# The opening of a gated, quantised feed-forward block: order of its loads, of one scale's range and of one weight tile's turns

## The chip, the cores and the metric

The kernel runs on one core of one Trainium2 chip. A core has a matrix engine (TensorE, PE in the profile), a vector engine (VectorE, DVE), a scalar engine for activation functions (ScalarE, ACT), a general engine (GpSimd, POOL) and SyncE (SP), which here only issues transfers. The engines run their own instruction streams in order and wait for each other through semaphores; transfers (DMA) run on 16 DMA engines of the core and are issued from the queue of SP or ACT. The metric is the time of one execution in microseconds (us) on the device, lower is better.

## The reference

x is (4, 1024, 512), cond is (4, 128); the weights are norm_w (512, 128), up_w (4096, 512) and down_w (512, 2048). All is float32.

```python
scale = cond @ norm_w.T + 1.0
ms = jnp.mean(x * x, axis=-1, keepdims=True)
h = x * (scale[:, None, :] * jax.lax.rsqrt(ms + EPS))
u = h @ up_w.T
val, gate = jnp.split(u, 2, axis=-1)
h = val * jax.nn.gelu(gate, approximate=False)
hq = act_quant(h)        # per token: round(h * 127 / max|h|), scaled back
wq = weight_quant(down_w) # round(w / mean|w|) in {-1, 0, 1}, scaled back
y = hq @ wq.T
return y + x
```

(`act_quant` and `weight_quant` stand in the reference inside a stop_gradient form, which leaves these values.) So each of the four batches has a scale per feature from its own row of cond; each token has a root of its mean square; the product with up_w is in full float32 precision, the product with down_w is of small whole numbers.

## The kernel before

**Products.** The up product is made of float16 parts: every float32 operand is brought into range by a power of two and split into a high and a low float16, and three of the four cross products are added in PSUM. Batches 1 to 3 use a seven-product scheme on 2 x 2 blocks (L474); batch 0, with which the kernel starts, uses the plain product (`plain`, L489, and for its very first block `plain_first`, L531), since the sums of weights that the scheme needs are made on the way. up_w is handled in 16 tiles W0 to W15 of 128 gate rows and 128 value rows. A tile is loaded (`w_load`, L248), its rows' largest values are brought to a power of two (`w_range`, L253 to L258), the rows are scaled (`w_scale`, L267 or L269), turned by TensorE against the identity (`w_turn`, L277, four 128 x 128 blocks per half) and split into high (`w_high`, ScalarE, L290 to L293) and low (`w_low`, VectorE, L299 to L302). `w_evac` (L306) keeps a float32 copy for the sums. The gate half of a tile goes ahead of its value half.

**The start.** The first half of batch 0 is four tiles of 128 tokens, `X0`. SP issues, in this order, two loads of two x tiles each (L705), W0 and W1 as four loads, two more pairs of x tiles, W2. ScalarE's queue issues cond, as one row of 4 x 128 numbers (L697), and norm_w (L698). Then:

- TensorE spreads cond's row over 128 partitions by a product with ones (`cond_spread_rows`, L159), into two PSUM tiles: the first batch's 128 numbers, and the other 384, which ScalarE copies to `cb` (L774) for a later use (`cond_scale_rest`, L175).
- VectorE multiplies norm_w by the first batch's row and adds along it, feature block by feature block (`cond_scale`, L164), adds 1 (L180) and takes the largest magnitude per partition (`cond_largest`, L182). `cond_over` turns this column into a row on TensorE (pm, L189), `cond_range` makes a power of two of its maximum on VectorE (L195 to L199), `cond_spread` brings that back to all partitions on TensorE (pd, L205). `cond_undo` (L209, L210) keeps it as `dx` and its reciprocal as `ux`, and `cond_bring_first` (L213) applies `ux` to the scale.
- ScalarE makes the sums of squares of the four x tiles (`first_sum`, L716) and the square root (L723); VectorE makes the reciprocal and one Newton step (`rsqrt_start`, L724 to L728). ScalarE scales tiles 0, 1 and 2 by it (`first_scale`, L733), VectorE tile 3 (L735). TensorE turns them, four blocks per tile, into four PSUM banks ptx (`first_turn`, L740). ScalarE writes the high half of each bank times the scale (`first_high`, L744), VectorE the low half (`first_low`, L748).
- Between these, TensorE runs products of zeros (`keep_warm`, pz, L756): six ahead of the spread, five behind it, five behind pm.
- Then `plain_first` runs 24 products of 512 columns for W0, in an order written out by hand, and calls `second_part` ahead of the seventh (W0's value rows turned and split, W1 scaled, the low halves of x, the load of the GELU table) and `second_slot` ahead of the seventeenth (W1 turned, W2 ranged and scaled).

Behind it come the other W tiles against both halves of batch 0, and then batches 1 to 3, whose vector and scalar work is placed by a small planner with costs (`Filler`, `SLOT_US`); the down products of a batch run among the up products of the next.

**What sets the order.** The program is recorded under a manual schedule: each engine runs its instructions in the order in which the lines above call them, so an instruction that waits holds up all that its engine has behind it. SP's loads are issued in order as well. PSUM has eight banks; pz, pm, pd and one ptx bank share the two banks of the tag "A".

Of the kernel before, what the change touches and what calls it, by code (L numbers as in the profile page):

```python
# [13 lines left out]
ALU = mybir.AluOpType  # L14
# [3 lines left out]
P = 128  # L18
# [23 lines left out]
def glu_quant_kernel(  # L42
# [10 lines left out]
    PE, ACT, DVE, POOL, SP = nc.tensor, nc.scalar, nc.vector, nc.gpsimd, nc.sync  # L53
    B, S, D = x.shape
    C = cond.shape[1]
# [3 lines left out]
    NA = TOK // P  # L59
    NK = D // P  # L60
    NJ = FF // P
    xf = x.flatten_outer_dims()
# [13 lines left out]
    ones = one.to_broadcast([P, P])  # L76
# [8 lines left out]
    H = cpool.tile([P, NSLOT, 2, TOK], F32, name="H")  # L85
# [10 lines left out]
    for n in range(0, P, 32):  # L96
        c = slice(n, n + 32)
# [35 lines left out]
    def pow2_floor(t):  # L133

        ti = t.bitcast(I32)
        DVE.tensor_scalar(ti, ti, EXPONENT, None, ALU.bitwise_and)

    def bank(tag, bufs, shape=None, name=None):
        return psum.tile(shape or [P, TOK], F32, name=name or tag, tag=tag, bufs=bufs)

    def po_bank(name, shape=None):
        return bank("po", 3, shape, name)


    scT = cpool.tile([P, NK, B], F32, name="scT")
    dx = cpool.tile([P, B], F32, name="dx")
    ux = cpool.tile([P, B], F32, name="ux")
    nw = R[:, 1, 0:512].rearrange("p (k c) -> p k c", k=NK)
    cb = R[:, 1, 512:1024].rearrange("p (b c) -> p b c", b=B)
    dots = R[:, 1, 1024 : 1024 + C]  # L150
    junk = R[:, 1, 2048:4096].rearrange("p (n d) -> p n d", d=D)

    cn = H[0:1, 3, 0, : B * C]

    def cond_spread_rows():

        pc = [bank("B", 1, name="pc_0"), bank("E", 2, name="pc_1")]
        for n, c in enumerate((slice(0, C), slice(C, B * C))):
            PE.matmul(pc[n][:, : c.stop - c.start], ones[:1, :], cn[:, c], start=True, stop=True)  # L159
        return pc  # L160

    def cond_scale(b, rows):
        for k in range(NK):
            DVE.scalar_tensor_tensor(  # L164
                dots, nw[:, k], 1.0, rows[:, :C], ALU.mult, ALU.mult, accum_out=scT[:, k, b : b + 1]
            )
# [11 lines left out]
    def cond_largest(b0, b1):  # L178
        v = scT[:, :, b0:b1]
        DVE.tensor_scalar(v, v, 1.0, None, ALU.add)  # L180
        mx = sm.tile([P, B], F32, name=f"mx_{b0}", tag="mx")[:, : b1 - b0]
        DVE.tensor_reduce(  # L182
            mx, v.rearrange("p k b -> p b k"), AX.X, ALU.max, apply_absolute_value=True
        )
        return mx

    def cond_over(mx, b0, b1, tag):
        pm = bank(tag, {"po": 3}.get(tag, 2), [B, P], f"pm_{b0}")[: b1 - b0]
        PE.transpose(pm, mx, ident)  # L189
        return pm  # L190

    def cond_range(pm, b0, b1):
        n = b1 - b0
        d4 = sm.tile([B, 1], F32, name=f"d4_{b0}", tag="d4")[:n]
        DVE.tensor_reduce(d4, pm, AX.X, ALU.max)  # L195
        DVE.tensor_scalar(d4, d4, 1e-30, None, ALU.max)
        pow2_floor(d4)
        dg = sm.tile([B, B], F32, name=f"dg_{b0}", tag="dg")[:n, :n]
        DVE.tensor_scalar(dg, ident[:n, :n], d4, 1.0 / X_UP, ALU.mult, ALU.mult)  # L199
        return dg  # L200

    def cond_spread(dg, b0, b1, tag):
        n = b1 - b0
        pd = bank(tag, {"po": 3}.get(tag, 2), [P, B], f"pd_{b0}")[:, :n]
        PE.matmul(pd, ones[:n, :], dg, start=True, stop=True)  # L205
        return pd

    def cond_undo(pd, b0, b1):
        DVE.tensor_copy(dx[:, b0:b1], pd)  # L209
        DVE.reciprocal(ux[:, b0:b1], dx[:, b0:b1])  # L210

    def cond_bring_first():
        DVE.tensor_scalar(scT[:, :, 0], scT[:, :, 0], ux[:, 0:1], None, ALU.mult)  # L213

    def cond_rows():

# [20 lines left out]
    def wn(j):  # L237
        return H[:, W_SLOT[j % 3]]
# [7 lines left out]
    def w_load(j, ts=(1, 0)):  # L246
        for t in ts:
            SP.dma_start(out=wn(j)[:, t], in_=up_v[j][:, t])  # L248

    def w_range(j, t0=0, t1=2):  # L250
        t = slice(t0, t1)
        am = sm.tile([P, 2], F32, name=f"wam_{j}_{t0}", tag="wam")[:, t]
        DVE.tensor_reduce(am, wn(j)[:, t], AX.X, ALU.max, apply_absolute_value=True)  # L253
        pow2_floor(am)
        DVE.tensor_scalar(sw[:, j, t], am, 2.0**-100, 1.0 / W_UP, ALU.max, ALU.mult)
        if j not in iv:
            iv[j] = sm.tile([P, 2], F32, name=f"iv_{j}", tag="iv", bufs=3)
        DVE.reciprocal(iv[j][:, t], sw[:, j, t])  # L258

    def w_gain(j):  # L260
        DVE.tensor_scalar(sg0[:, j, :], sw[:, j, :], dx[:, 0:1], None, ALU.mult)

    def w_scale(j, ts=(1, 0), eng=POOL):
        for t in ts:
            w, r = wn(j)[:, t], iv[j][:, t : t + 1]
            if eng is ACT:
                ACT.activation(w, w, AF.Copy, scale=r)  # L267
            else:
                eng.tensor_scalar(w, w, r, 1.0, ALU.mult, ALU.mult)  # L269

    def w_turn(j, banks=None, ts=(1, 0)):
        if j not in pw:
            pw[j] = banks or [po_bank(f"pw_{j}_{t}") for t in (1, 0)]
        for t in ts:
            n = 1 - t
            for k in range(NK):
                PE.transpose(  # L277
                    pw[j][n][:, k * P : (k + 1) * P], wn(j)[:, t, k * P : (k + 1) * P], ident
                )
# [414 lines left out]
    start_t = sm.tile([P, 1], F32, name="start_t", bufs=1)  # L694
    eps = sm.tile([P, 1], F32, name="eps", bufs=1)
    DVE.memset(eps, EPS)
    ACT.dma_start(out=cn, in_=cond.rearrange("(o b) c -> o (b c)", o=1))  # L697
    ACT.dma_start(out=nw, in_=norm_w.rearrange("(k p) c -> p k c", p=P))  # L698
    ACT.activation(start_t, one, AF.Sqrt)


    X0 = H[:, 4:8].rearrange("p s h d -> p (s h) d")

    def first_load(n):
        SP.dma_start(  # L705
            out=X0[:, n : n + 2],
            in_=xf[n * P : (n + 2) * P, :].rearrange("(s p) d -> p s d", p=P),
        )

    ssq0 = sm.tile([P, 8], F32, name="ssq0", bufs=1)  # L710
# [2 lines left out]
    def first_sum(n, eng=ACT):  # L713
        v, j, a = X0[:, n], junk[:, n % 4], ssq0[:, n : n + 1]
        if eng is ACT:
            ACT.activation(j, v, AF.Square, accum_out=a)  # L716
        else:
            eng.scalar_tensor_tensor(j, v, 1.0, v, ALU.mult, ALU.mult, accum_out=a)

    def rsqrt_start(t, y):  # L720

        z = sm.tile([P, NA], F32, name="newton", bufs=1)
        ACT.activation(z, t, AF.Sqrt, scale=1.0 / D, bias=eps)  # L723
        DVE.tensor_scalar(t, t, 1.0 / D, EPS, ALU.mult, ALU.add)  # L724
        DVE.reciprocal(y, z)
        DVE.tensor_tensor(z, y, y, ALU.mult)
        DVE.scalar_tensor_tensor(z, z, -0.5, t, ALU.mult, ALU.mult)
        DVE.scalar_tensor_tensor(y, z, 1.5, y, ALU.add, ALU.mult)  # L728
# [8 lines left out]
    def first_turn(n, pts):  # L737
        for k in range(NK):
            c = (n % NA) * P
            PE.transpose(pts[k][:, c : c + P], X0[:, n, k * P : (k + 1) * P], ident)  # L740

    def first_high(h, k, pt):
        c = slice(h * TOK, (h + 1) * TOK)
        ACT.activation(XP[:, 0, k, c], pt, AF.Copy, scale=scT[:, k, 0:1])  # L744
# [7 lines left out]
    def keep_warm(n):  # L752

        pz = bank("A", 2, name="pz")
        for i in range(n):
            PE.matmul(pz, warm[:, :P], warm, start=True, stop=True)  # L756

    first_load(0)
    first_load(2)
    w_load(0)  # L760
    w_load(1)
    first_load(4)
    first_load(6)
    w_load(2)
    keep_warm(6)
    pc = cond_spread_rows()
    keep_warm(5)
    for n in range(NA):
        first_sum(n)
    cond_scale(0, pc[0])  # L770
    mx = cond_largest(0, 1)
    pm = cond_over(mx, 0, 1, "A")
    rsqrt_start(ssq0[:, 0:NA], rs0[:, 0:NA])
    ACT.copy(cb[:, 1:].rearrange("p b c -> p (b c)"), pc[1][:, : (B - 1) * C])  # L774
    keep_warm(5)
    for n in (0, 1, 2):
        first_scale(n, ACT)
    first_scale(3, DVE)
    dg = cond_range(pm, 0, 1)
    w_range(0, 1, 2)  # L780
    w_scale(0, (1,), DVE)
    ptx = [po_bank(f"ptx_0_{k}") for k in range(3)] + [bank("A", 2, name="ptx_0_3")]
    first_turn(0, ptx)
    first_turn(3, ptx)
    pd = cond_spread(dg, 0, 1, "A")
    first_turn(1, ptx)
    first_turn(2, ptx)
    cond_undo(pd, 0, 1)
    cond_bring_first()
    w_turn(0, [bank("E", 2, name=f"pw_0_{t}") for t in (1, 0)], (1,))  # L790
    w_high(0, (1,))
    first_high(0, 0, ptx[0])
    w_range(0, 0, 1)
    w_low(0, (1,))
    w_scale(0, (0,), DVE)
    w_gain(0)
    first_high(0, 1, ptx[1])
    first_high(0, 2, ptx[2])
    first_high(0, 3, ptx[3])
    w_range(1)  # L800
    w_gain(1)
    w_scale(1, (0,))
# [142 lines left out]
    mx = cond_largest(1, B)  # L945
# [26 lines left out]
    pm = cond_over(mx, 1, B, "po")  # L972
    dg = cond_range(pm, 1, B)
# [178 lines left out]
    b = B - 1  # L1152
# [125 lines left out]
```

## Time and profile before

| | us |
|---|---|
| three runs, median | 752.07 |
| lowest, highest | 751.36, 752.24 |
| the profiled execution | 752.28 |
| its span, first to last instruction | 750.5 |
| TensorE busy | 741.7 |
| VectorE, ScalarE, GpSimd busy | 549.4, 377.5, 199.4 |
| norm_w's issue on ScalarE's queue, start | 1.29 |
| first instruction that uses norm_w (L164), start | 7.68 |
| square root of the sums (L723), start | 7.41 |
| x's turns (L740), first start | 11.81 |
| W0's gate rows' turns (L277), start | 15.10 |
| first product (L531), start | 16.97 |
| first GELU (L536), start | 23.82 |

The times of this table below the line of busy times are counted from the span's start. Each line of the profile names an engine, a line of the kernel, an operation and the tiles that it writes and reads; "idle before" is the time that the engine stood still ahead of an instruction and what ended it. An "x8" behind an instruction merges eight of them. "issue" is time in which nothing that the profile shows was waited for. The time of an execution is its span and about 1.8 us around it.

### The profile page before, as it was taken

The numbers are of one execution on the slowest core, as the hardware profiler recorded it, in microseconds if no ns is written. First come the engines' busy times: TensorE is split into PE (matmuls) and PEld (weight loads), VectorE is DVE, ScalarE is ACT, GpSimd is POOL, SyncE is SP. The second block draws the span as 40 slices with busy tenths as digits, with TensorE's granted clock in tenths as the row PEclk, the third lists the DMA queues.
The fourth block names the chain that finished last, engine by engine and source line by source line (L and its number), as shares of the span: only waits on it lengthen the run. The fifth ranks groups of instructions, "written<-read, shape, count | busy, mean of one in ns | idle before, by whom it ended". The sixth has DMA issues, their size and how long they took to land.

```text
span 750.5 us, 9573 instructions
## 1 busy us (share of the span) xinstructions
PE 741.7 (99%) x3484; PEld 344.9 (46%) x3484; DVE 549.4 (73%) x795; ACT 377.5 (50%) x618; POOL 199.4 (27%) x218
## 2 busy tenths in 40 slices
PE   7999999999999999999999999999999999999997
PEld 3554455454444444444444444444444444444443
DVE  5868688897989885545679886444778887445896
ACT  5758455656235655543434656443433666332274
POOL 0389577899010030332010030333020000000200
PEclk9999999999999999999999999999999999999999
DMA  6279649777622433666832415466823333333243
GB/s 224 71 260 233 195 156 226 202 195 172 202 84 99 130 124 119 183 204 146 228 103 98 127 64 182 137 190 179 197 99 102 109 114 109 107 99 112 88 152 112
DMA packets 94074, 111.28 MB, mean 148 GB/s; under 512 B 61382, under 2 KB 61894, under 8 KB 94028
## 3 DMA queue, kind: packets, MB, share of 16 engines
q1 hardware_dynamic: 93498, 110.42, 49.9%
q8 instruction: 27, 0.44, 0.3%
q10 hardware_dynamic: 530, 0.26, 0.1%
q14 instruction: 19, 0.16, 0.1%
HBM read 74.47 MB, written 23.09 MB: 130 GB/s over the span
## 4 chain that ended last, share of the span: by engine, by line
PE 93%; DVE 2%; ACT 2%; DMA 1%; POOL 1%; issue 1%; ACTq 0%; SPq 0%; DVEq 0%; POOLq 0%
PE A L474 32%; PE E L474 16%; PE po L682 11%; PE pg L489 9%; PE pv L489 9%; PE B L474 8%; PE po_end L682 4%; PE pw L277 2%; DMA R<-in_L_cond_norm_w_dram 1%; DMA SXY<-s_dram 1%; PE ptx L740 1%; DVE R L748 0%; DVE H L175 0%; ACT djk L356 0%; POOL SXY L325 0%
## 5 line engine op out<-in xcount | busy, mean ns | idle before, releaser
L474 PEld LDWEIGHTS <-SXY 128*128 128x128 f16 x2016 | 197.0, 98 | 238.5 <-DMA SXY<-s_dram 1.3
L474 PE MATMUL A<-R,SXY 128*128 128x512 f16 x1152 | 264.9, 379 | 0.1
L474 PE MATMUL E<-R,SXY 128*128 128x512 f16 x576 | 140.0, 379 | 0.0
L568 DVE SCALAR_TENSOR_TENSOR H<-A,sg,t 128x512 f32<-128x512 f32 x48 | 36.0, 750 | 81.1 <-PE A L474 81.1
L579 ACT ACTIVATE t<-t,sg 128x512 f32<-128x512 f32 x48 | 34.5, 720 | 106.5 <-DVE t L578 106.5
L682 PE MATMUL po<-wd,R 128*128 128x512 bf16 x384 | 85.3, 379 | 0.0
L682 PEld LDWEIGHTS <-R 128*128 128x128 bf16 x512 | 50.1, 98 | 60.4
L656 DVE TENSOR_TENSOR H<-H,am 128x1024 f32<-128x1024 f32 x64 | 76.2, 1216 | 0.0
L617 POOL PARTITION_ALL_REDUCE am<-R x8 | 14.6, 1821 | 221.1 <-DVE R L603 221.1
L601 DVE TENSOR_REDUCE gm<-H 128x512 f32<-128x1024 f32 x56 | 69.0, 1233 | 2.5 <-DMA wd<-tn 1.5
L474 PE MATMUL B<-R,SXY 128*128 128x512 f16 x288 | 70.0, 379 | 0.0
L578 DVE TENSOR_TENSOR t<-E,t 128x512 f32<-128x512 f32 x48 | 32.6, 679 | 49.3 <-PE E L474 49.3
L383 POOL TENSOR_TENSOR rs<-ssq,neghalf 128x2 f32<-128x2 f32 (+1 forms) x13 | 9.6, 739 | 205.2 <-DVE ssq L382 205.0
L489 PE MATMUL pv<-R 128*128 128x512 f16 x246 | 61.6, 379 | 0.0
L489 PE MATMUL pg<-R,SXY 128*128 128x512 f16 x252 | 57.8, 379 | 0.5 <-ACT g L536 0.5
L489 PEld LDWEIGHTS <-SXY 128*128 128x128 f16 x378 | 37.0, 98 | 42.9 <-issue 0.8
L489 PEld LDWEIGHTS <-R 128*128 128x128 f16 x366 | 35.8, 98 | 41.9 <-DVE R L299 0.2
L565 ACT ACTIVATE t<-B,sg 128x512 f32<-128x512 f32 x48 | 33.0, 687 | 37.2 <-PE B L474 37.2
L664 ACT ACTIVATE H<-H 128x1024 f32<-128x1024 f32 x39 | 40.9, 1049 | 20.8 <-DVE H L656 20.8
L549 ACT COPY t<-A 128x512 f32<-128x512 f32 x48 | 28.0, 584 | 45.0 <-PE A L474 44.7
L560 ACT COPY v<-E 128x512 f32<-128x512 f32 x48 | 28.1, 586 | 32.1 <-PE E L474 29.3
L556 ACT COPY B<-A 128x512 f32<-128x512 f32 x48 | 27.4, 571 | 31.2 <-PE A L474 30.2
(155 smaller groups left out, 911.7 us busy)
## 6 DMA issues: line engine op xcount, KB each, us to landing
SXY<-s_dram SPq DMA_DIRECT2D x48, 640.0 KB, 3.9
SXY<-s_dram SPq DMA_DIRECT2D x48, 256.0 KB, 4.6
s_dram<-SXY SPq DMA_DIRECT2D x11, 896.0 KB, 5.4
H<-in_L_cond_up_w_dram SPq DMA_DIRECT2D x32, 256.0 KB, 4.3
xr<-in_x_dram SPq DMA_DIRECT2D x19, 256.0 KB, 4.5
out_dram<-xr SPq DMA_DIRECT2D x19, 256.0 KB, 2.2
s_dram<-R SPq DMA_DIRECT2D x5, 896.0 KB
H<-in_x_dram SPq DMA_DIRECT2D x8, 512.0 KB, 5.7
```

The costliest lines, as they stand in the source:

```text
L474: PE.matmul(o, s[:, w, k, :], tv[:, :, c, l, k, :], start=start and n == 0, stop=stop and n == len(TERMS) - 1, skip_group_check=True,)
L489: PE.matmul(ps, a[k // 2][:, w, k % 2, :], XP[:, l, k, h * TOK : (h + 1) * TOK], start=n == 0, stop=n == len(terms) - 1,)
L549: ACT.copy(cur["t2"], cur["A"])
L560: ACT.copy(cur["v"], cur["E"])
L565: ACT.activation(cur["t1"], pb, AF.Gelu, scale=gain(g, 1))
L568: DVE.scalar_tensor_tensor(h_half(g - 1, 0), prev["A"], gain(g - 1, 0), prev["t1"], ALU.mult, ALU.mult)
L578: DVE.tensor_tensor(prev["t2"], prev["E"], prev["t2"], ALU.add)
L579: ACT.activation(prev["t2"], prev["t2"], AF.Gelu, scale=gain(g - 1, 1))
L601: DVE.tensor_reduce(gm[0], v, AX.X, ALU.max, apply_absolute_value=True)
L656: DVE.tensor_tensor(v, v, r.to_broadcast([P, 2, TOK]), ALU.mult)
L664: ACT.activation(v, v, AF.Copy, bias=MAGIC)
L682: PE.matmul(po, q[:, h, j, a * P : (a + 1) * P], wd[:, j, :], start=j == 0, stop=j == NJ - 1,)
```

## The change

It has five parts.

1. norm_w is loaded from SP's queue, ahead of x, and no longer from ScalarE's.
2. The first four x tiles are loaded singly, four loads for two.
3. Only the first batch's row of cond is loaded at the start and spread by TensorE. The other three rows are loaded straight into `cb`, the same row to all 128 partitions, by a transfer that ScalarE issues behind its fourth `first_high` (`cond_load_rest`); the copy L774 goes.
4. The first batch's scale, its range (`cond_scale` to `cond_spread`) and pd stand in front of the sums of squares and the root. The warmers are three ahead of the spread, five behind it, two behind pm and five behind pd. `cond_undo` takes the reciprocal straight from PSUM and applies it there, ahead of the copy to `dx`, and stands in front of the scaling of W0's gate rows.
5. x's tiles are turned in the order 0, 3, 1, then W0's gate rows, then tile 2. W0's value rows are scaled by GpSimd and not by VectorE.

Behind these, every engine's instructions stand in the order in which they stood.

```diff
-    cn = H[0:1, 3, 0, : B * C]
-    def cond_spread_rows():
-        pc = [bank("B", 1, name="pc_0"), bank("E", 2, name="pc_1")]
-        for n, c in enumerate((slice(0, C), slice(C, B * C))):
-            PE.matmul(pc[n][:, : c.stop - c.start], ones[:1, :], cn[:, c], start=True, stop=True)
+    cn = H[0:1, 3, 0, :C]
+    def cond_load_rest():
+        v = cond[1:].rearrange("b c -> (b c)").partition_broadcast(P)
+        ACT.dma_start(out=cb[:, 1:].rearrange("p b c -> p (b c)"), in_=v)
+    def cond_first_row():
+        pc = bank("B", 1, name="pc")
+        PE.matmul(pc[:, :C], ones[:1, :], cn, start=True, stop=True)
         return pc
...
     def cond_undo(pd, b0, b1):
+        DVE.reciprocal(ux[:, b0:b1], pd)
+        if b0 == 0:
+            DVE.tensor_scalar(scT[:, :, 0], scT[:, :, 0], ux[:, 0:1], None, ALU.mult)
         DVE.tensor_copy(dx[:, b0:b1], pd)
-        DVE.reciprocal(ux[:, b0:b1], dx[:, b0:b1])
-    def cond_bring_first():
-        DVE.tensor_scalar(scT[:, :, 0], scT[:, :, 0], ux[:, 0:1], None, ALU.mult)
...
-    ACT.dma_start(out=cn, in_=cond.rearrange("(o b) c -> o (b c)", o=1))
-    ACT.dma_start(out=nw, in_=norm_w.rearrange("(k p) c -> p k c", p=P))
+    ACT.dma_start(out=cn, in_=cond[0:1])
+    SP.dma_start(out=nw, in_=norm_w.rearrange("(k p) c -> p k c", p=P))
...
-    first_load(0)
-    first_load(2)
+    for n in range(NA):
+        first_load(n)
     w_load(0)
     w_load(1)
-    first_load(4)
-    first_load(6)
+    first_load(4, 2)
+    first_load(6, 2)
     w_load(2)
-    keep_warm(6)
-    pc = cond_spread_rows()
+    keep_warm(3)
+    pc = cond_first_row()
     keep_warm(5)
+    cond_scale(0, pc)
+    mx = cond_largest(0, 1)
+    pm = cond_over(mx, 0, 1, "A")
     for n in range(NA):
         first_sum(n)
-    cond_scale(0, pc[0])
-    mx = cond_largest(0, 1)
-    pm = cond_over(mx, 0, 1, "A")
+    keep_warm(2)
+    pd = cond_spread(cond_range(pm, 0, 1), 0, 1, "A")
+    keep_warm(5)
     rsqrt_start(ssq0[:, 0:NA], rs0[:, 0:NA])
-    ACT.copy(cb[:, 1:].rearrange("p b c -> p (b c)"), pc[1][:, : (B - 1) * C])
-    keep_warm(5)
     for n in (0, 1, 2):
         first_scale(n, ACT)
     first_scale(3, DVE)
-    dg = cond_range(pm, 0, 1)
     w_range(0, 1, 2)
+    cond_undo(pd, 0, 1)
     w_scale(0, (1,), DVE)
     ptx = [po_bank(f"ptx_0_{k}") for k in range(3)] + [bank("A", 2, name="ptx_0_3")]
-    first_turn(0, ptx)
-    first_turn(3, ptx)
-    pd = cond_spread(dg, 0, 1, "A")
-    first_turn(1, ptx)
+    for n in (0, 3, 1):
+        first_turn(n, ptx)
+    w_turn(0, [bank("E", 2, name=f"pw_0_{t}") for t in (1, 0)], (1,))
     first_turn(2, ptx)
-    cond_undo(pd, 0, 1)
-    cond_bring_first()
-    w_turn(0, [bank("E", 2, name=f"pw_0_{t}") for t in (1, 0)], (1,))
     w_high(0, (1,))
     first_high(0, 0, ptx[0])
     w_range(0, 0, 1)
     w_low(0, (1,))
-    w_scale(0, (0,), DVE)
+    w_scale(0, (0,))
     w_gain(0)
     first_high(0, 1, ptx[1])
     first_high(0, 2, ptx[2])
     first_high(0, 3, ptx[3])
+    cond_load_rest()
     w_range(1)
```

More of the change, by code (lines that the diff above doesn't have):

```diff
@@ L696, in glu_quant_kernel, with first_load @@
     DVE.memset(eps, EPS)
-    ACT.dma_start(out=cn, in_=cond.rearrange("(o b) c -> o (b c)", o=1))
-    ACT.dma_start(out=nw, in_=norm_w.rearrange("(k p) c -> p k c", p=P))
+    ACT.dma_start(out=cn, in_=cond[0:1])
+    SP.dma_start(out=nw, in_=norm_w.rearrange("(k p) c -> p k c", p=P))
     ACT.activation(start_t, one, AF.Sqrt)
     X0 = H[:, 4:8].rearrange("p s h d -> p (s h) d")
-    def first_load(n):
+    def first_load(n, m=1):
         SP.dma_start(
-            out=X0[:, n : n + 2],
-            in_=xf[n * P : (n + 2) * P, :].rearrange("(s p) d -> p s d", p=P),
+            out=X0[:, n : n + m],
+            in_=xf[n * P : (n + m) * P, :].rearrange("(s p) d -> p s d", p=P),
         )
```

## The prediction

> **What bounds the kernel now.** First the page, for the bound over the whole span. Part 1 gives each engine's busy time, part 2 the PE row in 40 slices of 18.8 us, in tenths:
>
> ```profile
> PE 741.7 (99%) x3484; PEld 344.9 (46%) x3484; DVE 549.4 (73%) x795; ACT 377.5 (50%) x618; POOL 199.4 (27%) x218
> PE   7999999999999999999999999999999999999997
> ```
>
> TensorE is idle only in the first slice and the last. Everything behind the start is a stream that PE sets, and what comes earlier at its head comes earlier at its end. So the question is when the first useful product (L531) starts. The diff edits nothing after it but one transfer and one scaling. Second, the chain of waits in that stretch (start, length, what; us):
>
> ```profile
> 1.29 6.28 DMA R<-in_L_cond_norm_w_dram
> ...
> 9.53 0.35 PE pm L189
> 9.88 2.13 PE pz L756 x5
> 12.02 1.71 PE ptx L740 x8
> 13.72 0.51 PE pd L205 x2
> 14.23 1.03 PE ptx L740 x8
> 15.27 0.45 PE pw L277 x4
> 15.72 0.02 issue
> 15.74 0.59 ACT SXY L290
> 16.33 0.60 ACT R L744
> 16.92 0.04 issue
> 16.97 1.75 PE pg L531 x6
> ```
>
> It begins with a transfer, norm_w, landed at 7.57. VectorE then makes the first batch's scale and its maximum (7.68 to 9.37), PE turns it (pm), fills with five warmers (pz), and turns sixteen x blocks around pd and four weight blocks; ScalarE splits the gate rows and the first x block, and the product starts at 16.97. Third, the waits up to 24 us (who waited for whom: total, times, longest), which confirm the late one:
>
> ```profile
> DVE R L164 <- DMA R<-in_L_cond_norm_w_dram: 4.6, 1, 4.6
> ACT SXY L290 <- PE pw L277: 3.6, 1, 3.6
> PE pg L531 <- ACT R L744: 1.3, 1, 1.3
> PE pm L189 <- DVE rs L725: 1.1, 1, 1.1
> ```
>
> Fourth, the timeline for x (L716 sums of squares), the root's consumers (L733), the DMA issues, and one slack that matters below:
>
> ```profile
> 0.72 0.96 SPq L705 DMA_DIRECT2D H<-in_x_dram  x2
> 1.29 0.43 ACTq L698 DMA_DIRECT2D R<-in_L_cond_norm_w_dram  x1
> 4.27 0.63 ACT L716 ACTIVATE R<-H 128x512 f32<-128x512 f32 x1 [1.03 <-DMA H<-in_x_dram]
> 6.05 0.63 ACT L716 ACTIVATE R<-H 128x512 f32<-128x512 f32 x1 [0.44 <-DMA H<-in_x_dram]
> 19.19 0.37 ACT L292 CAST R<-pw 128x256 f16<-128x256 f32 x1 [0.54 <-PE pw L277]
> ```
>
> **The change, part by part.**
>
> *norm_w to the front of SP's queue.* Why was it late? The DMA queues between 1.7 and 4.6 us (packets, MB, share) say it:
>
> ```profile
> q1 hardware_dynamic: 434, 0.86, 81.8%
> q10 hardware_dynamic: 23, 0.01, 1.3%
> ```
>
> ScalarE's queue (q10) got nothing while SP's (q1) carried x. Here a rule of the Trainium skill speaks against the change: "DMA: Bandwidth & Descriptors", section on queues, rings and completion order, has each DMA engine go round-robin over the queues that have work. By it norm_w already had half the engines from about 2.5 us, its lateness would be its own, and moving it gains nothing (rival 3). The row shows 434 packets to 23, so I take the row. Landing: the first x pair, 0.52 MB, was issued at 0.72 and woke ScalarE at 4.27; at the 390 GB/s of these microseconds its bytes are 1.34, leaving 2.2 fixed. norm_w's 512-byte rows are slower: 530 packets of q10 took 7.2% of the first 13 us, 0.94. So 0.72 + 2.2 + 0.94 = **3.85**, 3.7 earlier.
>
> *x singly, behind it.* SP issues seven DMAs where four stood up to W0 (0.48 each, so x3 at 2.6 and W0 at 3.1 instead of 1.7), which costs nothing while the data queue is full, and it is: by the same windows the engines move 340 to 400 GB/s from 2.5 to 12 us. x tile n lands at 0.72 + 2.2 + 0.94 + 0.67(n+1): 4.5, 5.2, 5.9, 6.5; the older pair's landing by that sum would be 5.6 and was 6.05 with part of norm_w beside it, so I take 6.6 for the last. ScalarE's sum of the last tile and its read-out (0.73 before L723) end at 7.35, where they ended at 7.41 before: single tiles gain nothing in themselves, they pay for norm_w. W0's gate rows land by about 7.8 as before (same bytes ahead), needed at 9; W1 and W2 are not needed before 13.5. SP's third weight load no longer waits on norm_w (2.7 us of SP's queue, hidden).
>
> *The cond range in front of x's roots.* The spread of one row instead of four costs PE between 0.52 (a quarter of the columns) and 1.04 (half of the instructions) of the old 2.07; I take 0.8, after three warmers (1.43 + 1.28 = 2.7) and a hand-over: done at 3.6. VectorE's scale and maximum: 3.9 + 1.69 = 5.6. PE's five warmers (0.43 each) run 3.6 to 5.75, pm 0.37 to 6.1. VectorE's four small steps (10.55 to 11.41: 0.86) end at 7.05. PE: two warmers to 7.0, pd 0.51 to 7.6, five warmers to **9.75**, where x's turns start; before, 12.02. Gain so far 2.27. VectorE's roots start when the square root (0.30) ends, 7.65, and take 0.85 (9.28 to 10.11): 8.5. ScalarE then scales three tiles (0.65 each): 9.15, 9.8, 10.45; VectorE the fourth at 9.0. So PE's warmers, not the roots, are last by 0.6.
>
> *W0's gate rows between x's tiles.* VectorE: 9.0 + range 1.27 (11.34 to 12.61) + undo 0.53 (14.27 to 14.80) + scaling 0.49 = 11.3. PE: before, 1.71 + 1.03 for sixteen turns and 0.45 for the gate rows; twelve turns cost 1.71 + 0.51, so they end at 11.97, the gate rows at 12.42, the last x tile at 12.95. Taking pd out of this stretch gains 0.51. ScalarE's split of the gate rows (0.59 + 0.02) now runs beside the last turns: 12.44 to 13.05, the first x split to 13.65, product at **13.70**. That is 16.97 - 13.70 = 3.27: 2.27 + 0.51 + 0.5 from the overlap.
>
> *Moved off the path.* W0's value rows go to POOL: 0.70 by its row at 19.42 instead of 0.49 on VectorE; range done by 12.6, scaled by 13.4, wanted by PE at 15.3 behind six products. Cover 1.9; without it, 0.21. VectorE's 0.49 saved is upside in the next microseconds; I count nothing. ScalarE loses the copy L774 (0.46, hidden under a 2.07 wait). Its new load of the other rows issues between the fourth x split and L292, in the 0.54 idle shown; one issue was 0.53 and 0.43 there, so with the two hand-overs it costs 0 to 0.3 (a slower broadcast form), taken **0.08**. What queues behind is L292, and PE's value products wait on that with 0.04 to spare. The data are wanted near 36 us.
>
> *The clock, the unknown.* PE's turns cost 0.21 each up to 13.7 and 0.13 after (1.71 and 1.03 for eight), its warmers 0.43 against 0.22 for later 512-wide products: the array ran at half speed until about 14 us. The granted-clock row does not resolve this. The Trainium skill, "TensorE: Matmul & The Clock Gate", Part 1, wants a busy window of some 3.4 us, free-running, so the change of speed comes one to two windows after work becomes dense; before, dense from 9.68, faster at about 14. In the new order dense from 7.6, so between 11.0 and 14.4. Part 4 of the page says transposes do not count as busy; by that all 20 turns stay slow (gate rows done at 9.75 + 16 x 0.213 = 13.16, splits behind them, product at 14.45, gain 2.5) and the products start slow for another window. The trace disagrees: the speed rose among turns, 1.7 us after the last warmer. I take half the turns slow, as before, which is the sum above; the ends are 6 slow (gain 3.4) and 20 slow.
>
> Sum: 3.27 - 0.08 = 3.2. The profiled execution took 752.28 for a span of 750.5, so 749.1 and a span of 747.3; it stands 0.2 above the median of 752.07, hence **748.9**.
>
> **The rivals.**
>
> 1. *Turns slow to the end.* Gain 2.5, less up to 1.3 if the first 3 us of products are slow too (some 14 products, and PE waits for ScalarE's splits through the first six anyway): 749.6 to 750.9. For it: the window's phase is not in the program. Against: the density is no less than before.
> 2. *Slower: the array stays slow through the first product group.* pm, pd and the wait for the gate rows break the dense work. Place: L531, 24 products at 0.43 instead of 0.22 and 12 turns, 6.3, less 1.1 idle there, 5.2 lost against 2.4 won: 754.9. It decides from 12 slow products on (2.4/0.21). Against: the longest new gap is about 0.75 (12.95 to 13.70), and one of 1.26 before did not slow it.
> 3. *norm_w as late as before.* Landing N gives turns at N + 5.75 (VectorE 1.74, pm 0.37, range 0.9, pd 0.55, warmers 2.15) and the product at N + 9.7; with the old 6.28 from an issue ended at 1.2, N = 7.5, product at 17.2, 752.3. It eats the whole gain from N = 7.3 on. Against: the two DMA rows.
> 4. *Given back to ScalarE.* From L292 to the first GELU ScalarE runs without a gap, and PE waits for it (0.5 at L536). If the broadcast's issue holds it 0.5 to 1.5 longer, 749.4 to 750.4.
>
> **How the numbers follow.** The forecast 0.62 (own range 748.2 to 749.7), rival 1 0.20, rival 4 0.08, rival 3 0.05, rival 2 0.05. 0.2% is 1.5 us, what a measurement of this kernel can tell from nothing: faster means below 750.57. Faster: 0.62 + 0.16 + 0.08 = 0.86; same: 0.04 + 0.05 = 0.09; slower 0.05. The range holds the forecast with VectorE's upside (747.9) and most of rival 1 and rival 4 (750.9).
>
> **What would show it.** VectorE's first scale at about 3.9 instead of 7.68, pd before 8, x's turns from about 9.75, product at 13.4 to 14.5, and from there every later group earlier by the same amount, PE's idle 0.5 at L536 not grown. Wrong it would be with norm_w's wait still ending after 6, turns still 0.21 at the gate rows, a gap at L292, or 512-wide products at 0.43.

## The result, and the profile after

The changed kernel takes 750.06 us in the median of 21 runs (748.65 to 751.59), the kernel before 752.30 (751.36 to 752.93). The ratio is 0.997, with a 95% interval of 0.9963 to 0.9977: 2.24 us faster, where 3.2 were forecast. The profiled execution took 748.98 with a span of 747.0, against a forecast of 749.1 and 747.3 for one. So the execution that was profiled did as forecast, and the median did not; the runs of the changed kernel lie over 2.9 us, those of the kernel before over 1.6. That difference is what the experiments are about.

The page after, the same two rows as before:

```profile
PE 737.6 (99%) x3481; PEld 343.1 (46%) x3481; DVE 548.7 (73%) x794; ACT 376.7 (50%) x617; POOL 199.7 (27%) x219
PE   7999999999999999999999999999999999999998
```

The stream behind the start is as full as it was. The chain of waits of the changed kernel up to its first product (start, length, what):

```profile
1.77 4.30 DMA H<-in_x_dram
6.07 0.02 issue
6.10 1.35 ACT R L718 x4
...
8.18 0.31 ACT newton L725
...
9.18 0.17 DVE rs L730
9.35 0.02 issue
9.38 0.49 DVE H L737
9.86 0.61 DVE wam L255
...
11.42 0.41 DVE H L271
11.82 0.04 issue
11.87 0.67 PE pw L279 x4
...
13.01 0.37 ACTq L157
13.37 0.37 ACT R L746
13.75 0.04 issue
13.79 1.75 PE pg L533 x6
```

norm_w has gone from it. In its place stands x's landing (the second tile's: ScalarE stood idle 1.23 ahead of its sum at 6.10, and the sums of the third and fourth followed at its own pace), and behind that the sums of squares, the root, and VectorE's way from the root to W0's gate rows (tile 3 scaled, rows ranged, undo, rows scaled). The product starts at 13.79 instead of 16.97, 3.18 sooner; the forecast was 13.70. The waits up to 24 us (who for whom: total, times, longest) say the same:

```profile
ACT R L718 <- DMA H<-in_x_dram: 2.6, 2, 1.4
PE ptx L742 <- ACT H L735: 1.6, 1, 1.6
ACT SXY L292 <- PE pw L279: 1.2, 1, 1.2
PE pg L533 <- ACT R L746: 0.8, 1, 0.8
PE pd L208 <- DVE dg L202: 0.4, 1, 0.4
```

TensorE itself now stands idle 1.6 us ahead of x's turns, waiting for ScalarE's scaling. In the kernel before no such wait is there; its warmers ran up to the turns. The timeline of the changed kernel (start, length, engine, line, operation):

```profile
3.65 0.29 DVE L167 SCALAR_TENSOR_TENSOR R<-R,pc 128x128 f32<-128x128 f32 x1 [0.58 <-PE pc L162]
4.14 0.63 ACT L718 ACTIVATE R<-H 128x512 f32<-128x512 f32 x1 [1.37 <-DMA H<-in_x_dram]
7.42 0.63 ACT L718 ACTIVATE R<-H 128x512 f32<-128x512 f32 x1
10.15 1.53 PE L742 MATMUL ptx<-ident,H 128*128 128x128 f32 x12 [1.64 <-ACT H L735]
16.01 0.37 ACT L294 CAST R<-pw 128x256 f16<-128x256 f32 x1 [0.54 <-PE pw L279]
```

The scale starts at 3.65, released by TensorE and no longer by norm_w. Twelve turns take 1.53, so the array was at full speed by then. The last tile's sum starts at 7.42 (before: 6.68).

### The profile page after: what moved, and what is told of

Same layout as the page of the kernel before. It is cut to its first block, busy times and chain, and to the rows that moved or that the text cites. A ratio compares the mean times of both kernels' runs of the same rounds, so it can differ in the third digit from the quotient of the medians.

```text
span 747.0 us, 9574 instructions
## 1 busy us (share of the span) xinstructions
PE 737.6 (99%) x3481; PEld 343.1 (46%) x3481; DVE 548.7 (73%) x794; ACT 376.7 (50%) x617; POOL 199.7 (27%) x219
## 4 chain that ended last, share of the span: by engine, by line
PE 96%; DVE 1%; ACT 1%; DMA 1%; issue 0%; SPq 0%; ACTq 0%; DVEq 0%
PE A L476 33%; PE E L476 16%; PE po L684 11%; PE pg L491 11%; PE pv L491 10%; PE B L476 8%; PE po_end L684 4%; PE pw L279 2%; DMA H<-in_x_dram 1%; DVE gm L603 0%; PE ptx L742 0%; PE pg L533 0%; ACT R L718 0%; ACT L813 0%; ACT H L308 0%
## 5 line engine op out<-in xcount | busy, mean ns | idle before, releaser
L476 PE MATMUL A<-R,SXY 128*128 128x512 f16 x1152 | 264.8, 379 | 0.0
```

The costliest lines, as they stand in the source:

```text
L476: PE.matmul(o, s[:, w, k, :], tv[:, :, c, l, k, :], start=start and n == 0, stop=stop and n == len(TERMS) - 1, skip_group_check=True,)
```

## The experiments

The kernels ran in three groups, each on one chip with the kernel before beside it: e1 to e4 (before: median 751.60), e5 to e8 (751.86), e9 to e12 (751.82). The kernel before itself differs by up to 0.7 us between chips (752.30 beside the result), so medians are compared within a group, and between groups the ratios. Two theories were opposed. One: what is missing from the median is the array's clock, which falls back to half in the opening of some runs. The other: it is x's landing, which varies.

**e1: norm_w back on ScalarE's queue, the rest changed.**

```diff
-    SP.dma_start(out=nw, in_=norm_w.rearrange("(k p) c -> p k c", p=P))
+    ACT.dma_start(out=nw, in_=norm_w.rearrange("(k p) c -> p k c", p=P))
```

> The changed kernel with norm_w's load back on ScalarE's queue, all else changed. Theory (norm_w was late because x held the DMA engines): its first user starts at 7 us or later, x's turns at about N + 5.75 = 13, the first product near 17; 752 to 753. Rival (each queue gets its share of the engines, norm_w is late for its own reasons): first user at 4 to 5, first product still near 14, 750 as the changed kernel.

Median 750.55 (749.51 to 752.31), ratio 0.9987 (0.9978 to 0.9996). Both missed. In its profile norm_w landed at 6.09, between the two, and the first product started at 16.08. Its DMA queues between 1.7 and 4.6 us:

```profile
q1 hardware_dynamic: 315, 0.58, 62.8%
q10 hardware_dynamic: 454, 0.23, 26.1%
```

Here the two queues share the engines. In the kernel before the same stretch had 434 packets to 23, but it ends as norm_w's packets begin; from 4.6 to 7.6 us the queues share there too:

```profile
q1 hardware_dynamic: 449, 0.83, 74.6%
q10 hardware_dynamic: 506, 0.25, 30.0%
```

So the difference is when norm_w's packets begin, at about 4.4 us before and 3.4 here, with its issue at 1.29 and 1.27. By then q1 had moved 0.79 MB before and 0.46 here; SP had issued two loads ahead of norm_w, 1.05 MB of pairs and 0.52 MB of single tiles. That fits a start in the order of issue over both queues, which stays a reading: no run tests it by itself. A landing of 6.09 and a product at 16.08 lie 9.99 apart, where the prediction's path gave N + 9.7 with about half of the turns slow (twelve took 2.21 in its chain, the path 1.71 + 0.51). By the ratios 0.13% of a gain is kept, where the changed kernel has 0.30% above and 0.28 and 0.19% in its controls below: norm_w's place is worth a third to somewhat over a half of it, and the rest of the new order keeps the remainder. The controls ran on other chips and most of the intervals overlap, so a finer split is open.

**e2: x in pairs again, the rest changed.**

```diff
-    for n in range(NA):
-        first_load(n)
+    first_load(0, 2)
+    first_load(2, 2)
```

> The changed kernel with the first four x tiles loaded as two pairs again. Theory A (the start now hangs on the last x tile, and single loads leave the DMA engines partly idle from 3.5 to 4.5 us): the last tile's sum starts 0.3 to 0.5 us before 7.42, first product near 13.4, median 0.3 to 0.5 us below the changed kernel's 750.06, the same 3 us of spread. Theory B (the spread of 3 us between runs comes from x's landing): the spread falls under 1 us and the median to 749. Rival (single tiles help as the change means them to): 0.3 us or more slower.

Median 751.70 (749.53 to 752.66), ratio 0.9999 (0.999 to 1.0008): the gain is gone. The rival was right about the sign. In the profile the pairs' first sums start at 5.65 and 8.56 and the last tile's at 9.19, against 8.14 and 7.91 with single tiles on the same chip (e3, e4), and the product starts at 16.27. TensorE stood idle 3.42 ahead of x's turns, the clock fell, and nine of the eleven runs have a mean clock of 0.998 or less. The prediction gave single tiles no value of their own; with norm_w in front the gain needs them. Why the second pair landed only at 8.5 no view shows: the engines were busy, at 250 to 266 GB/s from 4.5 to 6.5.

**e3: more warmers.**

```diff
     pd = cond_spread(cond_range(pm, 0, 1), 0, 1, "A")
-    keep_warm(5)
+    keep_warm(8)
...
     first_turn(2, ptx)
+    keep_warm(2)
     w_high(0, (1,))
```

> The changed kernel with three more warmers behind pd (eight) and two behind the last x turn, so that TensorE idles less between 8.5 and 13.8 us. Theory (the runs above 749 are those in which the array's clock falls back to half in the opening): spread under 1.5 us, median 749 to 749.5, granted clock at 0.999 or more in nearly all runs. Rival (the spread has another cause): median 750.1 or up to 0.5 higher for the added work, spread unchanged near 3 us.

Median 749.60 (749.13 to 750.42), ratio 0.9976 (0.9967 to 0.9985), spread 1.3 us, granted clock 0.999 or 1.0 in 10 of 11 runs. The spread and the clock are as the clock theory had it. The median is 0.1 above its band and says little, since this chip is a quicker one: by ratio e3 is no lower than the changed kernel beside the result (0.997). In this profile the last sum started 0.72 later than in the changed kernel's (8.14), the product 0.73 later (14.52), and the run took 749.81: landing varies and costs what it is late, but that isn't the 3 us.

**e4: no warmers behind pm and pd.**

```diff
-    keep_warm(2)
     pd = cond_spread(cond_range(pm, 0, 1), 0, 1, "A")
-    keep_warm(5)
```

> The changed kernel without the seven warmers behind pm and pd. Theory (clock): the array is at half speed when the turns and the first products run, so the first product starts 0.5 to 1 us later and the products take more; median 751 to 753. Rival (the warmers do not matter, the turns wait for ScalarE's scaling anyway): 750.1 or a little less.

Median 750.99 (750.12 to 751.41), ratio 0.9992 (0.9983 to 1.0001). At the edge of the clock theory's band, and 1.4 above e3 on the same chip. Its twelve turns took 2.82 (half speed; 1.53 in the changed kernel's profile), the product started at 15.58. Between e4 and e3 lie only warmers, which compute nothing. In this profile the clock did not fall, it had not yet risen: the row of the granted clock reads 1.00 from 7 to 19 us, while the turns took twice their time.

**e5 and e12: the changed kernel again, as controls.**

> The changed kernel itself once more, beside which the other kernels of this group are read. Both theories: 2 to 2.5 us under the kernel before on the same chip, runs spread over some 3 us.

> The changed kernel itself, beside which the others of this group are read: 2 to 2.5 us under the kernel before, with single runs 1 us or more above its median.

e5: 749.77 (749.03 to 751.19, 6 runs), ratio 0.9972, 2.1 us under the kernel before. e12: 750.57 (748.96 to 751.28, 12 runs), ratio 0.9981, only 1.25 under it, where 2 to 2.5 were expected. Both profiles are of runs above their median, and in both the clock fell. The stretches of e12 (busy time of each engine, then the granted clock PEclk, the DMA engines' share and GB/s):

```profile
7.00:9.00 2.00, 1.56 (x7) 0.70 (x7) 0.00 (x0) 0.74 (x3) 0.00 (x0) 1.00 1.00 367
9.00:11.00 2.00, 0.04 (x1) 0.04 (x1) 1.55 (x7) 1.10 (x3) 0.00 (x0) 0.73 1.04 400
11.00:13.00 2.00, 2.00 (x10) 2.00 (x11) 1.86 (x9) 1.13 (x2) 0.00 (x0) 0.50 0.99 373
13.00:15.00 2.00, 2.00 (x11) 2.00 (x10) 0.69 (x4) 0.33 (x1) 0.69 (x1) 0.50 0.06 22
15.00:17.00 2.00, 1.59 (x7) 0.62 (x6) 1.71 (x3) 2.00 (x5) 0.00 (x0) 0.56 0.50 146
17.00:19.00 2.00, 1.97 (x12) 0.99 (x11) 1.60 (x7) 1.34 (x4) 0.69 (x1) 1.00 0.37 84
```

The clock was full up to 9.93 (stretches of 0.5 us: 1.00, then 0.93, then 0.50), fell while TensorE had 0.04 us of work in two, and stayed at half until 16.76, through all the turns and into the first products: 6.8 us. The product started at 15.90. e9, the kernel with more warmers on the same chip, in the first three of these stretches:

```profile
7.00:9.00 2.00, 1.96 (x10) 0.99 (x10) 0.00 (x0) 1.97 (x6) 0.00 (x0) 1.00 0.92 337
9.00:11.00 2.00, 0.26 (x3) 0.02 (x1) 1.53 (x7) 1.09 (x3) 0.00 (x0) 1.00 1.05 405
11.00:13.00 2.00, 1.81 (x15) 1.57 (x16) 1.86 (x9) 1.16 (x2) 0.00 (x0) 1.00 1.06 394
```

Its eight warmers end at 9.24 (7.34 and 1.90), the other's five at 8.59, and the clock holds. The turns of the two (e12, then e9) start alike, late in both:

```profile
10.96 2.82 PE L742 MATMUL ptx<-ident,H 128*128 128x128 f32 x12 [2.36 <-ACT H L735]
10.98 1.53 PE L742 MATMUL ptx<-ident,H 128*128 128x128 f32 x12 [1.74 <-ACT H L735]
```

From there to the first product it is 4.94 in e12 and 3.64 in e9, as in the changed kernel's first profile (10.15 to 13.79). So the 2.11 by which e12's product is later than in that profile are 0.81 of later landing and 1.30 of clock. The two hang together: a late landing lengthens the idle time. In the profiles the clock held where TensorE stood idle 1.55 to 1.74 ahead of the turns (the changed kernel's first, e3, e8, e9, e10) and fell where it stood idle 1.91 to 3.42 (e5, e7, e12, e2). These are nine executions, and no threshold was measured.

Every run has its mean granted clock, so the 39 runs of the changed kernel can be sorted by it:

| mean granted clock of the run | runs | median us | lowest, highest |
|---|---|---|---|
| 1.000 | 11 | 749.37 | 748.65, 750.76 |
| 0.999 | 12 | 749.61 | 748.96, 750.08 |
| 0.998 | 4 | 750.52 | 750.06, 750.73 |
| 0.997 | 7 | 750.83 | 750.26, 751.46 |
| 0.995 | 5 | 751.19 | 751.12, 751.59 |

A half-speed stretch of 6.83 us is 6.83 x 0.5 / 749 = 0.0046 of the mean, the last row; half of it is 0.0023, the two rows above. The rows lie 1.8 us apart from first to last; by the two profiles above, some of that is the late landing that goes with a fall. The sorting works only where the clock has risen and falls again. Half speed ahead of the first change on record is not in this mean, which may be why the first row is wide, and in e4, whose profile shows just that, the runs at 0.995 have a lower median (750.66) than those at 1.000 (751.10).

**e6: norm_w's move alone, on the kernel before.**

```diff
-    ACT.dma_start(out=nw, in_=norm_w.rearrange("(k p) c -> p k c", p=P))
+    SP.dma_start(out=nw, in_=norm_w.rearrange("(k p) c -> p k c", p=P))
```

> The kernel before with one edit, norm_w's load from SP's queue in front of x. Theory (norm_w's bytes ahead of x push the last x tile back, and x's roots then bind in the old order): VectorE's first scale at 3.9, but the last sum of squares ends near 9 and x's turns start at 11.5 to 12.5, as before; within 0.5 us of the kernel before. Rival (norm_w's lateness was the whole loss): 2 us or more under it.

Median 751.70 (750.73 to 754.63), ratio 1.0003 (0.9992 to 1.0014). The median is the theory's, the reason isn't: in its profile the last sum began later than before (7.95), and yet the turns at 10.66 and the product at 15.42 began sooner (VectorE's first scale came at 4.93, held by TensorE's spread of cond). The runs fall apart instead, the lowest six at 750.73 to 751.45 and two, with a mean clock of 0.993, at 754.6. What the move wins, runs with a lower mean clock lose again.

**e7: W0's gate rows behind all four x tiles.**

```diff
-    w_turn(0, [bank("E", 2, name=f"pw_0_{t}") for t in (1, 0)], (1,))
     first_turn(2, ptx)
+    w_turn(0, [bank("E", 2, name=f"pw_0_{t}") for t in (1, 0)], (1,))
```

> The changed kernel with W0's gate rows turned behind all four x tiles. Prediction's step: the overlap is worth 0.5 us, so 0.5 above the changed kernel of this group. Rival (VectorE delivers the gate rows so late that TensorE has time for the last x tile first): 0 to 0.25 above it.

Median 749.64 (749.26 to 751.47), ratio 0.9976 (0.9968 to 0.9984); the control e5 has 749.77 and 0.9972 (0.9961 to 0.9983). The runs resolve no difference. Among those with a mean clock of 0.999 or more the medians are 749.56 (nine runs) and 749.66 (five), so 0.5 is unlikely. The profile after would leave some 0.3, as an estimate: TensorE waits 0.19 for the gate rows (ahead of L279 at 11.87), and one tile's turns take 0.51 (1.53 for three).

**e8 and e10: a shorter chain from the root.** With e3's warmers, the undo stands ahead of the root, where VectorE waits, and tile 3 is scaled behind the gate rows; e10 is e8 without the two warmers behind the last turn.

```diff
+    cond_undo(pd, 0, 1)
     rsqrt_start(ssq0[:, 0:NA], rs0[:, 0:NA])
     for n in (0, 1, 2):
         first_scale(n, ACT)
-    first_scale(3, DVE)
     w_range(0, 1, 2)
-    cond_undo(pd, 0, 1)
     w_scale(0, (1,), DVE)
+    first_scale(3, DVE)
...
-    for n in (0, 3, 1):
+    for n in (0, 1):
         first_turn(n, ptx)
     w_turn(0, [bank("E", 2, name=f"pw_0_{t}") for t in (1, 0)], (1,))
-    first_turn(2, ptx)
+    for n in (2, 3):
+        first_turn(n, ptx)
+    keep_warm(2)
```

> The kernel with more warmers (eight behind pd, two behind the last turn) and two steps taken off VectorE's chain from the root to W0's gate rows: the undo stands ahead of the root, where VectorE waits (0.45 us), and the scaling of x tile 3 behind that of the gate rows (0.49 us); x tiles turn in the order 0, 1, gate rows, 2, 3. Theory (the chain x's landing, root, VectorE, gate rows sets the start): first product 0.7 to 0.95 us after the root's place less, median 0.7 to 0.95 us under the kernel with more warmers alone, near 748.7. Rival (TensorE's turns or its clock set the start): no difference from it beyond 0.3.

> The kernel with the shortened VectorE chain, without its two warmers behind the last turn. Theory (those two are last before the first product there, 0.43 us of TensorE): first product 0.2 to 0.4 us sooner, median 0.2 to 0.4 under that kernel's, near 748.9. Rival (without them the clock falls in some runs): quick runs sooner by that, but single runs 1 us or more later.

e8: 749.18 (749.07 to 749.52, 5 runs), ratio 0.9962 (0.995 to 0.9974). e10: 749.17 (748.89 to 749.34, 5 runs), ratio 0.9965 (0.9953 to 0.9977). These are the lowest ratios and the narrowest spreads of all, though of five runs each. Against e3 the ratio is 0.0014 lower, 1.05 us, where 0.7 to 0.95 were expected, though on another chip; against e9, within e10's group, 0.2 us, and there the intervals overlap. In e8's profile the last sum starts at 7.91 and the product at 13.67, 5.76 later; in the changed kernel 7.42 and 13.79, 6.37 later; e10 has 5.76 and e9 6.37 as well. So the chain is shorter by 0.6, with x landing later. The two tail warmers make no difference that the runs or these profiles resolve.

**e9: e3's kernel again, beside e12.**

> The kernel with eight warmers behind pd and two behind the last turn once more, on the same chip as the changed kernel of this group. Theory (clock): the quick runs are no quicker than the changed kernel's quick runs, the runs that it has above 751 are gone, so the highest falls by 1 us or more and the median by 0.2 to 0.5. Rival (chance of a chip): spread as wide as the changed kernel's.

Median 749.39 (749.22 to 750.17, 6 runs), ratio 0.997 (0.9959 to 0.9981), e12 750.57. The highest fell by 1.1, the median by 1.2, more than expected, though the intervals of the two ratios still overlap (e12: 0.9972 to 0.999), and e9 has six runs for twelve. No run of e9 lies above 750.5, six of e12 do. What more warmers do to the clock is clearer than what they do to the median: with eight behind pd (e3, e8, e9, e10) one run of 27 has a mean clock of 0.998 or less, with five (the changed kernel and e7) 19 of 51. By ratio e3 and e9 (0.9976 and 0.997) are not clearly below the changed kernel (0.997, 0.9972, 0.9981).

**e11: norm_w between x tiles 1 and 2.**

```diff
     for n in range(NA):
+        if n == 2:
+            SP.dma_start(out=nw, in_=norm_w.rearrange("(k p) c -> p k c", p=P))
         first_load(n)
```

> The changed kernel with norm_w's load between x tiles 1 and 2 in SP's queue instead of in front. Theory (x's last landing binds, and the scale's path has more than 1 us to spare at full clock): the last sum of squares starts within 0.2 us of the changed kernel's, the first scale about 1.3 us later, the time is the same within 0.4. Rival (the small rows of norm_w at the head of the queue are what holds x back): the last sum 0.5 us or more sooner and the time 0.5 or more under it. Rival 2 (the scale's path binds): 1 us or more slower.

Median 751.01 (749.48 to 752.32), ratio 0.9991 (0.9982 to 1.0); e12 0.9981 (0.9972 to 0.999). A little slower, between theory and second rival. norm_w's landing moved by 2.4 us or more, not 1.3: it landed at 6.06, its user started at 6.14, and the product at 16.01 (N + 9.9 once more, with slow turns). At 2.4 late the scale's path binds again. The last sum began at 7.69, 0.54 before e12's, as the first rival had it, but the time did not follow. The wait for x moved with norm_w: here ScalarE waits 1.80 for the third tile, the one behind norm_w, where in the changed kernel's first profile it waits 1.37 and 1.23 for the first and second. And the landing is that of e1 (6.09), where norm_w stood behind the same two tiles in order of issue, but in the other queue.

## Why the prediction was right or wrong

Its own steps, in order.

- *norm_w at 3.85, the scale at 3.9, pd at 7.05.* Right: the scale at 3.65, pd at 6.95. Rival 3 fell.
- *"ScalarE's queue (q10) got nothing while SP's (q1) carried x."* Too strong. The row stops at 4.6 us; behind it the two queues share, and in e1 they share from about 3.4. What holds is that norm_w's packets began late.
- *The formula N + 9.7.* Right as the length of the scale's path with a slow array: 9.99 in e1, 9.95 in e11.
- *"Costs nothing while the data queue is full", so x's sums end at 7.35.* Wrong. The square root started at 8.18 here and at 8.5 to 9.0 in e3, e5, e8, e9 and e12. The engines weren't full: from 3.5 to 5.0 us they moved 262 GB/s, before 398. The second tile was to land at 5.2, and its sum began at 6.10. Mis-sized term: 0.8 to 1.6 us. What thins the traffic was not found; e5, e6, e7 and e8 show it too (189 to 320 GB/s in half-microsecond steps of that stretch), and in e11 ScalarE's wait moved with norm_w to the third tile.
- *"PE's warmers, not the roots, are last by 0.6."* Wrong, by that term: the roots are last by 1.64, and TensorE stands idle. The five warmers behind pd were counted as cover up to the turns; at full clock they take 1.25 and end at 8.51, while the turns start at 10.15. From this step comes the missing microsecond, in two parts: the later the landing, the later the product, and where the idle time grew to 1.91 (e5) and 2.36 (e12), the clock fell. Beside the result the 12 runs with a mean clock of 0.999 or more have a median of 749.42, the nine others 750.70.
- *"The density is no less than before", so at worst the turns are slow, 0.20.* Wrong in its reason. It looked only for a late rise. In the changed kernel the clock can rise as early as 6 us, and falls again in the wait ahead of the turns. In the profiles of e5 and e12 the half-speed stretch covers x's first twelve turns, in e12 the first products too; 16 of 39 runs have a mean clock (0.998 or less) that such a stretch gives. Slow turns are rival 1's loss, though not by its late rise, and its band of 749.6 to 750.9 is where the median lies. Its 0.20 should have been near 0.4, by 16 of 39.
- *Rival 2, slow products.* Not in the changed kernel, but perhaps in e6: two runs, which have no profile, took 754.6 with a mean clock of 0.993. That this is near the 754.9 worked out for another kernel is chance; by its own terms that sum is 6.1 and not 6.3, so 754.7.
- *The overlap of 0.5.* Not seen in e7; by the trace some 0.3. That the profiled execution met its forecast (13.79 for 13.70) was luck, since errors cancel: roots 0.8 late and VectorE's gate rows 0.55 late (11.87 for 11.3) against a clock that was full ahead of the turns instead of halfway through them.
- *GpSimd's scaling and ScalarE's load at no cost or 0.08.* Right as far as the trace goes: GpSimd was done at 13.79, TensorE wanted the rows at 15.37; the idle 0.54 ahead of the value rows' split is unchanged.
- *Everything behind the product comes earlier by the same.* Right: the first GELU 3.18 sooner (23.82 to 20.64), and the groups behind take what they took (L474's 1152 products into A 264.9, now 264.8).

The median lies within the range (747.9 to 750.9), 1.16 above the forecast of 748.9. Parts 3 and 5 of the change, the other rows of cond and the value rows on GpSimd, were not run by themselves, so what they are worth is open.

## What to carry to other kernels

When one transfer is moved to the head of a queue, the wait goes to what it passed; follow that one to the end of its own chain before calling it hidden, and ask what then covers the idle time. Filler work that holds a clock belongs where the engine will wait after the change, not where it waited before: the same change with ten warmers for five lost its tail of runs near 751 (none of 17). And where a median misses and one profile fits, sort the runs by what each of them records (here the mean clock) before looking for a cause in the one trace, and check that the record covers the stretch in question (in e4 it did not).

## What the runs showed of the hardware that was not expected

- The array's clock was full from about 6 us in the changed kernel's profile (its two warmers behind pm took 0.59, in e12 0.87), after some 4.5 us of warmers with short breaks, and fell to half in e12 within 1.4 us after TensorE had gone idle (8.59 to 9.93). The stretch at half then lasted 6.8 us there, although the turns ran without a gap from 10.96. In the kernel before, 7 us of warmers and of cond's spread (1.43 to 8.41) had not brought it up: the last of these warmers were still 0.43 apart.
- The page's row of the granted clock shows full speed also ahead of the first change on record: in the kernel before it reads 1.00 from 1 to 13 us, while the warmers cost 0.43 and the turns 0.21, twice their later cost. Durations, not the row, tell the clock in a program's first microseconds.
- A load issued on a second queue at the same time (1.29 and 1.27) began to move at about 4.4 us behind two loads of 512 KB, and at about 3.4 behind two of 256 KB; from then on the two queues shared the DMA engines (506 packets to 449, and 454 to 315). In one and the same place in the order of issue it landed at 6.09 from the second queue (e1) and at 6.06 from the first (e11). These are single executions; what decides it stays open.
